# A graph-attention and expert kernel: expert jobs as one list over all passes, and weights loaded with whole rows per partition

## The chip, the cores and the metric

The kernel runs on one core of a Trainium2 chip. A core has a matrix engine (TensorE, PE in the profile; its weight loads are PEld), three further engines (VectorE or DVE, ScalarE or ACT, GpSimd or POOL), a queue engine that only issues transfers (SyncE or SP), and 16 DMA engines that move data between the chip's memory (DRAM here) and the core's own memory. Matrix results land in a small accumulator memory (PSUM). Each engine works through its own instructions in order and waits at semaphores for the others. The metric is the device time of one execution in microseconds (us); lower is better.

## The reference, cut to what matters

A graph layer is followed by a layer of eight experts. There are 6,250 nodes of 256 values, 100,000 edges, 8 experts with weights of 256 x 1024 and 1024 x 256 and a capacity of 977 nodes each. All is float32.

```python
h = layernorm(x)
messages = (h @ W_forward.T)[src] * direction[:, 0:1] + (h @ W_reverse.T)[src] * direction[:, 1:2]
scores = leaky_relu(einsum('ef,hf->eh', messages, attn), 0.2)
e = exp(scores - scores.max(0))
norm = e / (segment_sum(e, dst)[dst] + 1e-10)
x = x + concat_heads(segment_sum(messages * norm[:, hd:hd+1], dst))

t = layernorm(x)
probs = softmax(t @ gate_w + gate_b);  idx = argmax(probs);  prb = max(probs)
pos = number of earlier nodes with the same expert;  kept = pos < C
buf[idx, pos] = t                                   # only where kept
hmid = relu(einsum('ecd,edf->ecf', buf, w1) + b1)
ybuf = einsum('ecf,efd->ecd', hmid, w2) + b2
x = x + nan_to_num(ybuf[idx, pos] * prb * kept)
```

The order of the 256 inner values (`d`) and of the 1024 middle values (`f`) plays no part in the two expert products, as long as both factors of a product use the same order.

## The kernel before, in words

**Edge phase.** The edges, sorted by target node, are cut into 131 groups of 6 x 128, two groups to a batch, 66 batches. For batch `b`, `gathers` (POOL) fetches a row of `node_tab` for every edge, three batches ahead; `messages` (DVE, and one exp on ACT) forms the messages and the exponentials, `products` (DVE) multiplies them, and `windows` (PE) sums them by target with a 0/1 matrix as the stationary operand; the sums are stored by SP. When a chunk of four node tiles is complete, `route` normalises it, adds it to `x`, computes the layer norm and the gate, and gives each node a row in its expert's part of `buf`; POOL later scatters the rows there.

**Experts.** The rows of each expert come in five passes of 128, 256, 256, 256 and 128 rows (`PASS`), so that experts can begin before all nodes are routed: pass 0 when its nodes are scattered, and so on. A job is one pass of one expert; there are 40. `experts(p)` is a generator for one pass: it fetches rows and both weight matrices of experts 0 and 1, then for each expert

- `columns` turns the rows `xe` with PE transposes into `xT` (L1188, through `px`);
- `ph` (L1211): w1's columns are the stationary operand, `xT` is the moving one, 16 products per job; ACT adds the bias `b1t`, applies relu and writes `hf` (L1214);
- rows and w1 of the expert two further on are fetched (`fetch_rows`, `fetch_w1`), and the columns of the next expert are made;
- `py` (L1225): `hf` is the stationary operand, w2 the moving one; then w2 of the expert two further on is fetched (`fetch_w2`), DVE adds `b2` and cleans NaNs, and SP stores `y` to `ybuf`.

The two last experts of a pass fetch nothing; the first fetches of the next pass are in its own generator. `w1t` and `w2t` have two buffers each. Every matrix product in float32 shows as two matmul and weight-load pairs in the profile, so `ph` of a job is 32 pairs.

**Order.** The schedule is written out by hand: the main loop over batches calls `messages`, `windows`, a share of expert pieces, `products`, `windows`, a share, `route` pieces and `gathers` in turn. `step_experts` takes pieces from the generators of started passes until a credit of 4.3 us is used up; each `yield` gives the cost of a piece. After the last batch (near 1704 us) all remaining passes are worked off in one loop; after every third piece it fetches outputs (`fetch_outputs`: POOL gathers `ybuf` rows for two node tiles, SP loads the residual `xr`) and finishes earlier ones (`finish`: ACT, DVE and a store by SP). The outputs of a pass's nodes are fetched once the following pass is done.

**Layouts.** The layout of w1 in `fetch_w1` is

```python
w1[e].rearrange("(c p) f -> p c f", p=P)   # partition p holds rows p and 128+p, 4 KB each
w2[e].rearrange("(c p) d -> p c d", p=P)   # partition p holds rows p, 128+p, ...: 8 rows of 1 KB
```

so the stationary operand of `ph`, `w1t[:, d, f * P:(f + 1) * P]`, is 128 neighbouring values in each partition. The biases `b1` are loaded as 64 rows of 128 and transposed on PE to `b1t`, with one column per expert and block of 128 middle values.

Of the kernel before, what the change touches and what calls it, by code (L numbers as in the profile page):

```python
# [8 lines left out]
F32 = mybir.dt.float32  # L9
I32 = mybir.dt.int32  # L10
AF = mybir.ActivationFunctionType
# [3 lines left out]
P = 128  # L15
# [504 lines left out]
def kernel(  # L520
# [27 lines left out]
    nc = tc.nc  # L548
    N, D = x.shape
# [307 lines left out]
    nc.scalar.dma_start(gb, bass.AP(tensor=gate_b.tensor, offset=gate_b.offset, ap=[[0, P], [1, E]]))  # L857
    b2b = ep.tile([P, E, D], F32, name="b2b")
    nc.scalar.dma_start(b2b, bass.AP(tensor=b2.tensor, offset=b2.offset, ap=[[0, P], [D, E], [1, D]]))
    b1t = ep.tile([P, E * FC], F32, name="b1t")  # L860
    with tc.tile_pool(name="pb1", bufs=1) as pb1, \
            tc.tile_pool(name="psb", bufs=1, space=bass.MemoryType.PSUM) as psb:
        b1n = pb1.tile([E * FC, P], F32, name="b1n")
        nc.scalar.dma_start(b1n, b1.rearrange("e (c p) -> (e c) p", p=P))
        pbt = psb.tile([P, E * FC], F32, name="pbt")
        nc.tensor.transpose(pbt, b1n, ident[:E * FC, :E * FC])
        nc.vector.tensor_copy(b1t, pbt)

        ii = pb1.tile([P, NT], I32, name="ii")
        nc.gpsimd.iota(ii[:, :E], pattern=[[-1, E]], base=E, channel_multiplier=0)  # L870
        rank = ep.tile([P, E], F32, name="rank")
        nc.vector.tensor_copy(rank, ii[:, :E])
        ij = pb1.tile([P, NT], I32, name="ij")
        nc.gpsimd.iota(ij, pattern=[[P, NT]], base=NSLOT, channel_multiplier=1)
        own = ep.tile([P, NT], F32, name="own")
        nc.vector.tensor_copy(own, ij)
        valid = ep.tile([P, NT], F32, name="valid")
        nc.vector.tensor_scalar(valid, own, float(NSLOT + N), None, op0=OP.is_lt)
# [23 lines left out]
    with tc.tile_pool(name="p2", bufs=2) as p2, tc.tile_pool(name="p4", bufs=1) as p4, \  # L902
# [94 lines left out]
        taken = {"before": None, "z": 0}  # L997

        def windows(b, g):

# [164 lines left out]
        def fetch_w1(e):  # L1165
            w1t = wpool.tile([P, DC, FF], F32, name="w1t")
            nc.sync.dma_start(w1t, w1[e].rearrange("(c p) f -> p c f", p=P))
            return w1t

        def fetch_w2(e):  # L1170
            w2t = wpool.tile([P, FC, D], F32, name="w2t")
            nc.sync.dma_start(w2t, w2[e].rearrange("(c p) d -> p c d", p=P))
            return w2t

        def fetch_rows(p, e):
            S = PASS[p]
            J = S // P
            a = e * TOT + OFF[p]
            xe = p5.tile([P, 2, D], F32, name="xe", bufs=3)[:, :J, :]
            x_loads.append(nc.sync.dma_start(xe, buf[a:a + S, :].rearrange("(p j) d -> p j d", j=J)))  # L1180
            return xe

        def columns(p, xe):
            J = PASS[p] // P
            px = ps2.tile([P, DC, 2 * P], F32, name="px")[:, :, :PASS[p]]
            for j in range(J):
                for d in range(DC):
                    nc.tensor.transpose(px[:, d, j * P:(j + 1) * P], xe[:, j, d * P:(d + 1) * P], ident)  # L1188
            xT = p5.tile([P, DC, 2 * P], F32, name="xT")[:, :, :PASS[p]]
            nc.scalar.copy(xT, px)  # L1190
            return xT

        def experts(p):

            S = PASS[p]
            J = S // P
            FB = 512 // S
            w1s, w2s, xs = {}, {}, {}
            for e in (0, 1):
                xs[e], w1s[e], w2s[e] = fetch_rows(p, e), fetch_w1(e), fetch_w2(e)  # L1200
            yield 0.0
            xT = columns(p, xs.pop(0))
            yield 0.43 * J
            for e in range(E):
                w1t, w2t = w1s.pop(e), w2s.pop(e)
                hf = p5.tile([P, FC, 2 * P], F32, name="hf")[:, :, :S]
                for f0 in range(0, FC, FB):
                    ph = ps2.tile([P, FB, S], F32, name="ph", tag="acc", bufs=3)
                    for f in range(f0, f0 + FB):
                        for d in range(DC):  # L1210
                            nc.tensor.matmul(ph[:, f - f0, :], w1t[:, d, f * P:(f + 1) * P], xT[:, d, :],  # L1211
                                             start=(d == 0), stop=(d == DC - 1))
                    for f in range(f0, f0 + FB):
                        nc.scalar.activation(hf[:, f, :], ph[:, f - f0, :], AF.Relu,  # L1214
                                             bias=b1t[:, e * FC + f:e * FC + f + 1])
                    yield 0.85 * FB * J
                if e + 2 < E:
                    xs[e + 2], w1s[e + 2] = fetch_rows(p, e + 2), fetch_w1(e + 2)
                if e + 1 < E:
                    xT = columns(p, xs.pop(e + 1))  # L1220
                    yield 0.43 * J
                py = ps2.tile([P, 2, D], F32, name="py", tag="acc", bufs=3)[:, :J, :]
                for j in range(J):
                    for f in range(FC):
                        nc.tensor.matmul(py[:, j, :], hf[:, f, j * P:(j + 1) * P], w2t[:, f, :],  # L1225
                                         start=(f == 0), stop=(f == FC - 1))
                    if j + 1 < J:
                        yield 3.4
                if e + 2 < E:
                    w2s[e + 2] = fetch_w2(e + 2)  # L1230
                y = p5.tile([P, 2, D], F32, name="y")[:, :J, :]
                nc.vector.tensor_add(y, py, b2b[:, e, :].unsqueeze(1).to_broadcast([P, J, D]))  # L1232
# [5 lines left out]
                nc.sync.dma_start(ybuf[a:a + S, :].rearrange("(p j) d -> p j d", j=J), y)  # L1238
                yield 3.4

        def settle(n0, n1):
# [43 lines left out]


        SHARE = 8.6
        routing, passes, todo = [], [], []
        held = []
        credit = 0.0  # L1290
        next_c, next_p = 0, 0
# [38 lines left out]
        started = {}  # L1330
        for b in range(NB + 1):
            for p in [p for p, at in started.items() if b >= at]:
                passes.append(experts(p))
                del started[p]
            if b < NSLOT // 512:
                clear(buf, 512 * b)
                clear(ybuf, 512 * b)
            if b < NB:
                messages(b)
            if b:  # L1340
                windows(b - 1, order[b - 1][0])
            step_experts(SHARE / 2)
            if b < NB:
                products(b)
            if b and len(order[b - 1]) > 1:
                windows(b - 1, order[b - 1][1])
            step_experts(SHARE / 2)
            while next_c < len(chunks) and done_at[next_c] < b:
                routing.append(routes_of(next_c))
                next_c += 1  # L1350
            step_routing(3)
            pool_work.extend(held)
            held = todo[:]
            del todo[:]
            if b + 3 < NB:
                gathers(b + 3)
            if not pool_work and not held and not todo:
                for p in wait_pass:
                    started[p] = b + 2
                del wait_pass[:]  # L1360
# [2 lines left out]
            step_routing(1)  # L1363
        for put in pool_work + held + todo:
            put()
        for p in list(started) + wait_pass:
            passes.append(experts(p))
        ends = [0] + [t for t in LASTS[:-1]] + [NT - 1]
        fetch = []
        for q in range(NP):  # L1370
# [3 lines left out]
        settle(1, EARLY + 1)  # L1374
        settle(EARLY + 1, NT)
        settle(0, 1)
        left = NP - len(passes)
        work = [t for q in range(max(left - 1, 0)) for t in fetch[q]]
        for q, gen in enumerate(passes):
            pieces = 0  # L1380
            for cost in gen:
                pieces += 1
                if pieces % 3 == 0:
                    if len(fetched) > 1 or fetched and not work:
                        finish()
                    if work:
                        fetch_outputs(work.pop(0))
            work += fetch[left + q - 1]
        for tiles in work + fetch[NP - 1]:
            if len(fetched) > 1:  # L1390
                finish()
# [58 lines left out]
```

## Time and profile before

| | us |
|---|---|
| median of 3 runs | 2086.88 (2086.45 to 2089.06) |
| profiled execution, its own time | 2076.85 |
| its span | 2075.1 |
| PE busy in the span | 1176.9 (57%) |
| PE weight loads | 971.2 (47%) |
| DVE busy | 969.5 (47%) |
| POOL busy | 841.0 (41%) |
| ACT busy | 288.2 (14%) |
| mean granted PE clock | 0.762 of full speed |
| moved by DMA | 248.03 MB, 119 to 120 GB/s in the mean |

Lines of the profile start with a time in us from the start of the span and a duration, or with a stretch; "L1211" is line 1211 of the kernel, and `out<-in` names the tiles written and read. "SPq" is a transfer issued by SP; a DMA in the chain of waits lasts from its issue to its landing. In square brackets stands how long the engine had been idle before, and what ended the wait. The ends of matmuls are modelled, so steady rates are read from a row of many in succession.

### The profile page before, as it was taken

What the parts mean: (1) busy time and instruction counts of PE and PEld (TensorE: products, weight loads), DVE (VectorE), ACT (ScalarE), POOL (GpSimd) and SP (SyncE); (2) the same over time, 40 slices, a digit from 0 to 9 for tenths busy, and PEclk for the clock granted to TensorE, in tenths of its full rate; (3) what the DMA queues carried; (4) which work ended last, traced back from release to release, by engine and by line L of the source; (5) the groups of instructions that cost most, each with busy time, mean ns of one, the idle gap of its engine ahead of it and who ended that gap; (6) DMA issues with size and microseconds to landing.
All of it is one profiled execution on the core that took longest, in us unless ns stands there. A gap on an engine that the chain in (4) does not pass through costs nothing.

```text
span 2075.1 us, 16070 instructions
## 1 busy us (share of the span) xinstructions
PE 1176.9 (57%) x5000; PEld 971.2 (47%) x5000; DVE 969.5 (47%) x2074; ACT 288.2 (14%) x755; POOL 841.0 (41%) x896
## 2 busy tenths in 40 slices
PE   6421345443443763646436666467556789899760
PEld 5320333332332652535325555355445678788650
DVE  7640455463463561636544566375454643131224
ACT  2100000010010110201011111110110123232221
POOL 0075655536626445353734355455355301010112
PEclk9755766766776875867657787688677889999995
DMA  6222343332222642522243343343332337384773
GB/s 208 83 58 67 99 119 116 118 110 60 61 64 62 202 136 65 175 77 75 67 126 103 105 134 103 97 112 106 89 107 54 114 111 252 137 273 147 245 234 112
DMA packets 164365, 248.03 MB, mean 120 GB/s; under 512 B 19971, under 2 KB 128014, under 8 KB 164142
## 3 DMA queue, kind: packets, MB, share of 16 engines
q1 hardware_dynamic: 131466, 176.86, 26.0%
q0 software_dynamic: 29728, 67.35, 13.6%
q10 hardware_dynamic: 3076, 2.69, 0.4%
q8 instruction: 42, 0.69, 0.1%
q14 instruction: 53, 0.43, 0.1%
HBM read 181.85 MB, written 64.98 MB: 119 GB/s over the span
## 4 chain that ended last, share of the span: by engine, by line
PE 20%; DVE 11%; issue 10%; DMA 7%; another core or an unknown queue 3%; ACT 1%; POOL 1%; SPq 0%; DVEq 0%; ACTq 0%; POOLq 0%
PE py L1225 8%; PE ph L1211 8%; PE pv L1009 3%; DMA part<-sums 2%; DMA w1t<-in_L_ffn_w_dram 2%; DVE v L992 1%; DMA yg<-ybuf,to_get 1%; DVE m L967 1%; DVE rv L965 1%; DMA out_dram<-o 1%; PE pv L1018 1%; DMA sums<-r 1%; DVE hot L982 1%; DVE gt L960 1%
## 5 line engine op out<-in xcount | busy, mean ns | idle before, releaser
L944 POOL DMA_INDIRECT gt<-node_tab,srci x782 | 740.8, 947 | 730.7 <-DVE sc L970 500.8
L1009 PE MATMUL pv<-v,hot 128*128 128x260 f32 x1564 | 460.1, 453 | 307.7 <-issue 149.5
L1009 PEld LDWEIGHTS pv<-v,hot 128*128 128x128 f32 x1564 | 356.5, 232 | 393.5 <-issue 204.5
L1225 PE MATMUL py<-w2t,hf 128*128 128x256 f32 x1024 | 258.5, 407 | 76.5 <-ACT hf L1214 52.8
L1211 PE MATMUL ph<-xT,w1t 128*128 128x256 f32 (+1 forms) x1280 | 261.8, 362 | 45.4 <-issue 29.5
L1211 PEld LDWEIGHTS ph<-xT,w1t 128*128 128x128 f32 x1280 | 226.5, 209 | 74.8 <-issue 44.0
L1225 PEld LDWEIGHTS py<-w2t,hf 128*128 128x128 f32 x1024 | 206.8, 206 | 115.7 <-ACT hf L1214 55.3
L992 DVE TENSOR_TENSOR v<-m,fixed 128x3072 f32<-128x3072 f32 (+1 forms) x66 | 218.7, 3314 | 8.0 <-remote 1.8
L982 DVE TENSOR_TENSOR hot<-fixed,local 128x1536 f32<-128x1536 f32 (+1 forms) x66 | 114.2, 1730 | 205.4 <-remote 137.6
L1018 PE MATMUL pv<-v,zt 128*128 128x260 f32 x226 | 83.2, 453 | 161.9 <-DVE zt L1017 122.8
L1265 POOL DMA_INDIRECT yg<-ybuf,to_get x49 | 49.4, 1009 | 289.3 <-DMA ybuf<-y 134.5
L1232 DVE TENSOR_TENSOR y<-py,b2b 128x512 f32<-128x512 f32 (+1 forms) x40 | 23.3, 583 | 305.8 <-PE py L1225 292.7
L1214 ACT ACTIVATE hf<-ph,b1t 128x256 f32<-128x256 f32 (+1 forms) x320 | 116.4, 431 | 331.7 <-PE ph L1211 236.9
L1018 PEld LDWEIGHTS pv<-v,zt 128*128 128x128 f32 x226 | 46.3, 218 | 179.1 <-DVE zt L1017 130.5
L1021 ACT COPY r<-pv 128x260 f32<-128x260 f32 x131 | 47.5, 368 | 536.3 <-issue 460.6
L1136 POOL DMA_INDIRECT buf<-h,to_put x49 | 48.6, 991 | 87.7 <-DVE kept L1158 73.1
L960 DVE TENSOR_TENSOR gt<-gt,fixed 128x816 f32<-128x816 f32 (+1 forms) x66 | 65.5, 993 | 34.5 <-DMA gt<-node_tab,srci 27.3
L967 DVE TENSOR_TENSOR m<-gt,rv 128x408 f32<-128x408 f32 x131 | 75.5, 576 | 4.6
L965 DVE TENSOR_TENSOR rv<-gt,fixed 128x408 f32<-128x408 f32 x131 | 76.2, 581 | 2.2
L991 DVE COPY fixed<-v 128x48 f32<-128x48 f32 (+1 forms) x66 | 13.8, 209 | 122.3 <-ACT v L980 89.6
L980 ACT ACTIVATE v<-sc 128x48 f32<-128x48 f32 (+1 forms) x66 | 16.0, 243 | 390.9 <-DVE sc L978 174.0
L920 PE MATMUL pm<-ident,top_s 128*128 128x128 f32 x56 | 12.0, 332 | 76.9 <-DVE top_s L926 57.8
(208 smaller groups left out, 860.7 us busy)
## 6 DMA issues: line engine op xcount, KB each, us to landing
w1t<-in_L_ffn_w_dram SPq DMA_DIRECT2D x40, 1024.0 KB
w2t<-in_L_ffn_w_dram SPq DMA_DIRECT2D x40, 1024.0 KB
sums<-r SPq DMA_DIRECT2D x113, 125.9 KB
gt<-node_tab,srci POOLq DMA_INDIRECT x782
buf<-zeros SPq DMA_DIRECT2D x16, 512.0 KB
ybuf<-zeros SPq DMA_DIRECT2D x16, 512.0 KB
part<-sums SPq DMA_DIRECT2D x12, 520.0 KB
x_d<-x SPq DMA_DIRECT2D x12, 512.0 KB
```

The costliest lines, as they stand in the source:

```text
L944: nc.gpsimd.indirect_dma_start(out=gts[b][:, i - i0, :], out_offset=None, in_=node_tab, in_offset=bass.IndirectOffsetOnAxis(ap=srci[:, i:i ...
L960: nc.vector.tensor_mul(fw, fw, fac[:, 0, :n].unsqueeze(2).to_broadcast([P, n, MS]))
L965: nc.vector.tensor_mul(rv[:, :k, :], gt[:, a0:a1, MS:ROW], fac[:, 1, a0:a1].unsqueeze(2).to_broadcast([P, k, MS]))
L967: nc.vector.tensor_add(m[:, a0:a1, :], fw[:, a0:a1, :], rv[:, :k, :])
L982: nc.vector.tensor_tensor(hot[:, :n, :], lane_p.unsqueeze(1).to_broadcast([P, n, P]), local[:, i0:i1].unsqueeze(2).to_broadcast([P, n, P]) ...
L992: nc.vector.tensor_mul(v[:, :n, 0:H * O].rearrange("p n (h o) -> p n h o", h=H), m[:, :n, 0:O].unsqueeze(2).to_broadcast([P, n, H, O]), w[ ...
L1009: nc.tensor.matmul(pv, hot[:, i - i0, :], v[:, i - i0, :], start=(i == tiles[0]), stop=(i == tiles[-1] and before is None))
L1018: nc.tensor.matmul(pv, z[:, k, :], before, start=False, stop=True)
L1211: nc.tensor.matmul(ph[:, f - f0, :], w1t[:, d, f * P:(f + 1) * P], xT[:, d, :], start=(d == 0), stop=(d == DC - 1))
L1214: nc.scalar.activation(hf[:, f, :], ph[:, f - f0, :], AF.Relu, bias=b1t[:, e * FC + f:e * FC + f + 1])
L1225: nc.tensor.matmul(py[:, j, :], hf[:, f, j * P:(j + 1) * P], w2t[:, f, :], start=(f == 0), stop=(f == FC - 1))
L1265: nc.gpsimd.indirect_dma_start(out=yg[:, n, :], out_offset=None, in_=ybuf, in_offset=bass.IndirectOffsetOnAxis(ap=to_get[:, n0 + n:n0 + n ...
```

## The change

There are five edits.

1. One generator `experts()` goes through all 40 jobs. Job `i` fetches w1 and w2 of job `i + 2` also across the border between passes. It waits (`yield None`) until the pass of its job is released; rows are fetched only for released passes (`taken["released"]`). The columns of the next job are made before `py` also across a border, if the rows have been fetched.
2. w1 and w2 are loaded so that partition `p` holds whole neighbouring rows: two rows of w1 (8 KB in one piece) and eight rows of w2 (8 KB in one piece).
3. To match, the stationary operands are taken with a step: `w1t[:, d, f::FC]` (step 8) for `ph` and `xe[:, j, d::DC]` (step 2) for the transposes. `hf` and w2 then agree without further steps.
4. `b1` is loaded directly into `b1t` with `b1.rearrange("e (p c) -> p e c", c=FC)`, without the transpose.
5. The first weights are fetched when experts are first called in the main loop, after batch 12; the outputs' loop counts pieces over all passes.

```diff
-    b1t = ep.tile([P, E * FC], F32, name="b1t")
-    with tc.tile_pool(name="pb1", bufs=1) as pb1, \
-            tc.tile_pool(name="psb", bufs=1, space=bass.MemoryType.PSUM) as psb:
-        b1n = pb1.tile([E * FC, P], F32, name="b1n")
-        nc.scalar.dma_start(b1n, b1.rearrange("e (c p) -> (e c) p", p=P))
-        pbt = psb.tile([P, E * FC], F32, name="pbt")
-        nc.tensor.transpose(pbt, b1n, ident[:E * FC, :E * FC])
-        nc.vector.tensor_copy(b1t, pbt)
+    b1t = ep.tile([P, E, FC], F32, name="b1t")
+    nc.scalar.dma_start(b1t, b1.rearrange("e (p c) -> p e c", c=FC))
+    with tc.tile_pool(name="pb1", bufs=1) as pb1:
...
+        jobs = [(p, e) for p in range(NP) for e in range(E)]
+        w1s, w2s, xs = {}, {}, {}
+
+        def fetch_w1(i):
+            if i < len(jobs):
+                w1s[i] = wpool.tile([P, DC, FF], F32, name="w1t")
+                nc.sync.dma_start(w1s[i], w1[jobs[i][1]].rearrange("(p c) f -> p c f", c=DC))
+
+        def fetch_w2(i):
+            if i < len(jobs):
+                w2s[i] = wpool.tile([P, FC, D], F32, name="w2t")
+                nc.sync.dma_start(w2s[i], w2[jobs[i][1]].rearrange("(p c) d -> p c d", c=FC))
+
+        def fetch_rows(i):
+
+            if i < len(jobs) and i not in xs and jobs[i][0] < taken["released"]:
...
-                    nc.tensor.transpose(px[:, d, j * P:(j + 1) * P], xe[:, j, d * P:(d + 1) * P], ident)
+                    nc.tensor.transpose(px[:, d, j * P:(j + 1) * P], xe[:, j, d::DC], ident)
...
-        def experts(p):
+        def experts():
+
+
+            for i in (0, 1):
+                fetch_w1(i)
+                fetch_w2(i)
+            xT = None
+            for i, (p, e) in enumerate(jobs):
...
+                while taken["released"] <= p:
+                    yield None
+                for q in (i, i + 1):
+                    fetch_rows(q)
+                if xT is None:
+                    xT = columns(i)
+                    yield 0.43 * J
...
-                            nc.tensor.matmul(ph[:, f - f0, :], w1t[:, d, f * P:(f + 1) * P], xT[:, d, :],
+                            nc.tensor.matmul(ph[:, f - f0, :], w1t[:, d, f::FC], xT[:, d, :],
                                              start=(d == 0), stop=(d == DC - 1))
...
-                if e + 2 < E:
-                    xs[e + 2], w1s[e + 2] = fetch_rows(p, e + 2), fetch_w1(e + 2)
-                if e + 1 < E:
-                    xT = columns(p, xs.pop(e + 1))
+                fetch_rows(i + 2)
+                fetch_w1(i + 2)
+                xT = None
+                if i + 1 in xs:
+                    xT = columns(i + 1)
                     yield 0.43 * J
...
-                if e + 2 < E:
-                    w2s[e + 2] = fetch_w2(e + 2)
+                fetch_w2(i + 2)
...
         def step_experts(share):
             nonlocal credit
             credit = min(credit + share, share)
-            while passes and credit > 0:
-                cost = next(passes[0], None)
+            while credit > 0 and b > 12:
+                cost = next(ffn, None)
                 if cost is None:
-                    passes.pop(0)
-                else:
-                    credit -= cost
+                    break
+                credit -= cost
...
-        for q, gen in enumerate(passes):
-            pieces = 0
-            for cost in gen:
-                pieces += 1
-                if pieces % 3 == 0:
-                    if len(fetched) > 1 or fetched and not work:
-                        finish()
-                    if work:
-                        fetch_outputs(work.pop(0))
-            work += fetch[left + q - 1]
+        work, pieces, counted = [], 0, 0
+        for cost in ffn:
+
+            while counted < taken["passes"] - 1:
+                work += fetch[counted]
+                counted += 1
+            pieces += 1
+            if pieces % 3 == 0:
+                if len(fetched) > 1 or fetched and not work:
+                    finish()
+                if work:
+                    fetch_outputs(work.pop(0))
+        for q in range(counted, NP - 1):
+            work += fetch[q]
```

More of the change, by code (lines that the diff above doesn't have):

```diff
@@ L995, in products @@
                 w[:, :n, :].unsqueeze(3).to_broadcast([P, n, H, O]))
-        taken = {"before": None, "z": 0}
+        taken = {"before": None, "z": 0, "released": 0, "passes": 0}
         def windows(b, g):
@@ L1163, in end_pass @@
             nc.vector.tensor_tensor(done, done, kept, OP.min)
[L1165 to L1186, printed above, removed]
+        jobs = [(p, e) for p in range(NP) for e in range(E)]
[8 more added lines that the diff above has]
+                nc.sync.dma_start(w2s[i], w2[jobs[i][1]].rearrange("(p c) d -> p c d", c=FC))
@@ new lines, in fetch_rows, with columns @@
+        def fetch_rows(i):
+            if i < len(jobs) and i not in xs and jobs[i][0] < taken["released"]:
+                p, e = jobs[i]
+                S = PASS[p]
+                J = S // P
+                a = e * TOT + OFF[p]
+                xs[i] = p5.tile([P, 2, D], F32, name="xe", bufs=3)[:, :J, :]
+                x_loads.append(nc.sync.dma_start(xs[i], buf[a:a + S, :].rearrange("(p j) d -> p j d", j=J)))
+        def columns(i):
+            S = PASS[jobs[i][0]]
+            xe = xs[i]
+            px = ps2.tile([P, DC, 2 * P], F32, name="px")[:, :, :S]
+            for j in range(S // P):
@@ L1187, in columns @@
                 for d in range(DC):
-                    nc.tensor.transpose(px[:, d, j * P:(j + 1) * P], xe[:, j, d * P:(d + 1) * P], ident)
-            xT = p5.tile([P, DC, 2 * P], F32, name="xT")[:, :, :PASS[p]]
+                    nc.tensor.transpose(px[:, d, j * P:(j + 1) * P], xe[:, j, d::DC], ident)
+            xT = p5.tile([P, DC, 2 * P], F32, name="xT")[:, :, :S]
             nc.scalar.copy(xT, px)
             return xT
-        def experts(p):
[L1195 to L1205, printed above, removed]
+        def experts():
[4 more added lines that the diff above has]
+            for i, (p, e) in enumerate(jobs):
+                S = PASS[p]
+                J = S // P
+                FB = 512 // S
+                while taken["released"] <= p:
[5 more added lines that the diff above has]
+                    yield 0.43 * J
+                w1t, w2t = w1s.pop(i), w2s.pop(i)
@@ L1210, in experts @@
                         for d in range(DC):
-                            nc.tensor.matmul(ph[:, f - f0, :], w1t[:, d, f * P:(f + 1) * P], xT[:, d, :],
+                            nc.tensor.matmul(ph[:, f - f0, :], w1t[:, d, f::FC], xT[:, d, :],
                                              start=(d == 0), stop=(d == DC - 1))
                     for f in range(f0, f0 + FB):
-                        nc.scalar.activation(hf[:, f, :], ph[:, f - f0, :], AF.Relu,
-                                             bias=b1t[:, e * FC + f:e * FC + f + 1])
+                        nc.scalar.activation(hf[:, f, :], ph[:, f - f0, :], AF.Relu, bias=b1t[:, e, f:f + 1])
                     yield 0.85 * FB * J
-                if e + 2 < E:
-                    xs[e + 2], w1s[e + 2] = fetch_rows(p, e + 2), fetch_w1(e + 2)
-                if e + 1 < E:
-                    xT = columns(p, xs.pop(e + 1))
+                fetch_rows(i + 2)
[3 more added lines that the diff above has]
+                    xT = columns(i + 1)
                     yield 0.43 * J
@@ L1238, in experts @@
                 nc.sync.dma_start(ybuf[a:a + S, :].rearrange("(p j) d -> p j d", j=J), y)
+                if e == E - 1:
+                    taken["passes"] = p + 1
                 yield 3.4
@@ L1287 @@
         SHARE = 8.6
-        routing, passes, todo = [], [], []
+        routing, todo = [], []
+        ffn = experts()
         held = []
@@ L1332 @@
             for p in [p for p, at in started.items() if b >= at]:
-                passes.append(experts(p))
+                taken["released"] = p + 1
                 del started[p]
@@ L1365 @@
             put()
-        for p in list(started) + wait_pass:
-            passes.append(experts(p))
+        taken["released"] = NP
         ends = [0] + [t for t in LASTS[:-1]] + [NT - 1]
@@ L1376 @@
         settle(0, 1)
-        left = NP - len(passes)
-        work = [t for q in range(max(left - 1, 0)) for t in fetch[q]]
-        for q, gen in enumerate(passes):
-            pieces = 0
-            for cost in gen:
-                pieces += 1
-                if pieces % 3 == 0:
-                    if len(fetched) > 1 or fetched and not work:
-                        finish()
-                    if work:
-                        fetch_outputs(work.pop(0))
-            work += fetch[left + q - 1]
+        work, pieces, counted = [], 0, 0
[11 more added lines that the diff above has]
+            work += fetch[q]
         for tiles in work + fetch[NP - 1]:
```

## The prediction

> **What bounds the kernel now.** I read the busy time by stretch first, then the chain of work that ended last, then the instructions in order of time around the places that the chain names. Stretches (start:end, length, busy us of PE, weight loads, DVE, ACT, POOL, then granted clock, DMA share, GB/s):
>
> ```profile
> 1704.00:1801.00 97.00, 97.00 (x450) 84.94 (x450) 25.83 (x74) 27.31 (x64) 8.68 (x9) 0.97 0.51 172
> 1801.00:1927.00 126.00, 117.44 (x546) 102.28 (x544) 27.82 (x49) 35.62 (x84) 11.55 (x12) 0.96 0.62 205
> 1927.00:2014.00 87.00, 65.06 (x400) 58.23 (x400) 22.77 (x49) 26.08 (x84) 12.72 (x12) 0.92 0.83 274
> ```
>
> From 1704 us to 2014 us only experts' jobs are left: the end of pass 2, pass 3 (256 rows a job) and pass 4 (128 rows). TensorE is full in the first two stretches; in the third it is not, and the DMA share is 0.83. Before 1704 us experts are filled in beside the edge phase, and TensorE is busy 55 to 62% there. The chain, at its two breaks and in between:
>
> ```profile
> 1794.33 6.92 PE py L1225 x32
> 1804.07 6.57 DMA w1t<-in_L_ffn_w_dram
> 1810.77 9.41 PE ph L1211 x32
> 1820.62 6.91 PE py L1225 x32
> 1827.53 6.91 PE ph L1211 x32
> ...
> 1919.95 6.92 PE py L1225 x32
> 1929.69 6.18 DMA w1t<-in_L_ffn_w_dram
> 1936.01 6.51 PE ph L1211 x32
> 1942.73 3.46 PE py L1225 x16
> 1946.19 3.58 PE ph L1211 x32
> ```
>
> A 256-row product of 32 matmul and weight-load pairs takes 6.91 us, 216 ns a pair; a 128-row `ph` takes 3.58 us, 112 ns a pair. A pass that starts waits for its first `w1t`, and its first `ph` then runs on a lowered clock (9.41 and 6.51 us). In pass 4 it is SP that is late:
>
> ```profile
> 1955.30 0.44 SPq L1172 DMA_DIRECT2D w2t<-in_L_ffn_w_dram  x1
> 1964.21 0.33 SPq L1238 DMA_DIRECT2D ybuf<-y  x1
> 1966.01 0.48 SPq L1180 DMA_DIRECT2D xe<-buf  x1
> 1966.59 0.38 SPq L1167 DMA_DIRECT2D w1t<-in_L_ffn_w_dram  x1
> ```
>
> The store of `y` (ready at 1955.4) leaves only at 1964.2, after the gathers of `ybuf` issued until 1958.7; rows and weights of later jobs stand behind it. From its first `ph` (1936.0) to its end (2013.8) pass 4 takes about 9.7 us a job, where TensorE needs 3.58 + 0.25 + 3.46 = 7.3.
>
> [...] The change makes the stationary operand of `ph` step 8 floats (32 bytes) and that of the transposes `px` 2 floats (8 bytes). [...] The trace shows 240 to 430 GB/s in single microseconds with either matrix in flight, so 1 KB rows of `w2` cost little, and longer rows alone move nothing large. Two views bear on the stride. Eight bytes in a weight load (`raw_a`, min/median/max) against none (`fs`), and DVE reductions without a step, then with 16 bytes:
>
> ```profile
> L766 PEld LDWEIGHTS pti<-ident,raw_a x14: 196/226/226, 85.9 to 90.5; 128*128 128x128 f32 x14
> L766 PEld LDWEIGHTS pti<-ident,fs x7: 182/225/231, 81.6 to 88.0; 128*128 128x128 f32 x7
> ...
> 95.97 0.95 DVE L806 TENSOR_REDUCE wrong<-local 128x1 f32<-128x782 f32 x1
> 97.78 0.27 DVE L810 TENSOR_REDUCE wrong<-high 128x1 f32<-128x131 f32 x1
> 714.91 0.33 DVE L926 TENSOR_REDUCE top_s<-gmax 128x4 f32<-128x104 f32 x1
> 1687.47 0.62 DVE L926 TENSOR_REDUCE top_s<-gmax 128x4 f32<-128x264 f32 x1
> ```
>
> Eight bytes cost nothing, so I cost `px` at nothing. DVE goes from (0.95-0.27)/651 = 1.04 ns an element to (0.62-0.33)/160 = 1.81 ns [...].
>
> **The change, part by part.** No run shows a weight load with 32 bytes of step[...] a pair takes about 229 ns. All sums are against the profiled execution's 2076.85 us (span 2075.1).
>
> *256-row `ph`.* (229-216) x 32 = 0.4 us a job; 15 such jobs run after 1704 us: **+6**. The cover is the matmul of 216 ns; without it each job costs more, as under the second rival.
>
> *Start of pass 3.* The end of `py` at 1801.25 to the end of the first `ph` at 1820.2 is 18.9 us; inside a pass `px` and `ph` take 7.3. Weights come two jobs ahead across the border and rows are there (all are released), so nothing is late and the clock stays up: **-11.6**.
>
> *Pass 4.* Now 87.0 us from 1926.87 to 2013.8. After: 8 x (32 x 0.229 + 0.25 + 3.46) = 88.3. The wait at its start goes and the slower loads fill its place. SP's store of `y` still waits for gathers and later `w1t` still stand behind it, but a job of 11 us gives more time than one of 9.7: I add 2 for it. **+3**.
>
> *Edge phase, pass 0.* (229-112) x 32 = 3.7 us x 8 jobs = 30 us of TensorE. Its cover is TensorE's idle time beside DVE and POOL, and it is not whole:
>
> ```profile
> 704.10 0.42 DVE L1232 TENSOR_TENSOR y<-py,b2b 128x256 f32<-128x256 f32 x1 [16.39 <-PE py L1225]
> ```
>
> Here DVE stands still for `py`, and the messages and products of the next edge batch are queued behind it; ACT's exp is likewise behind `hf`. Elsewhere (789 to 819 us) TensorE issues a matmul only every 1.7 to 2.4 us and the load vanishes in the gaps. I take 0.4 of it: **+12** (bounds 0 and 30). Pass 1 and the first job of pass 2: 9 x 0.4 x 0.4 = **+1.5**.
>
> *Starts of passes 0 to 2.* TensorE waited 2.05, 2.25 and 4.82 + 1.53 us for weights and rows. Weights of pass 0 are fetched far earlier (four loads, with the edge batches' stores behind them for a few us, while nothing waits for these stores). The transposes of pass 2's first job move two windows ahead. Of 10.6 us I take 0.6: **-6**.
>
> *Bias.* Before, a transpose and a copy on DVE wait for `b1n`:
>
> ```profile
> 101.94 0.34 PE L866 MATMUL pbt<-ident,b1n 64*128 64x64 f32 x1 [9.32 <-DMA b1n<-in_L_ffn_b_dram]
> 103.16 1.11 POOL L944 DMA_INDIRECT gt<-node_tab,srci  x1 [2.96 <-DVE lead L1150]
> ```
>
> The first gather waits for `lead`, which is behind that copy; 1.67 us of wait and the copy go: **-2**. The new load has 1024 pieces of 32 bytes, but is first read at about 697 us, so it costs nothing.
>
> *Fetching of outputs.* Pieces are counted over all passes instead of per pass: the same gathers, some one piece earlier or later; and the 61 us after the last `py` stay. 0.
>
> Sum: 6 - 11.6 + 3 + 12 + 1.5 - 6 - 2 = **+3**, so 2080 for the profiled execution. The median of the runs (2086.88) stands 10 above the profiled one; with the same 10 I forecast **2090**.
>
> **The rivals.**
> *The stride costs nothing.* For it: TensorE's weight load need not behave as DVE's reader; 8 bytes cost nothing. Against: [...] DVE's 1.81 ns. Then +6, +12 and +1.5 go; pass 4 is bound by DMA: 274 GB/s x 87 us = 24 MB now, 4 MB of it loaded earlier, 20 MB at 298 GB/s (its rate from 1936 to 2000) is 66 us, -21; if SP's waits hold it, only -10. In all -30 to -41: 2046 to 2057.
> *The loads outgrow the matmuls.* One mechanism, in the same place, which ends slower: from a load of about 216 ns every further ns is paid in each of the 15 x 32 pairs of full TensorE as well; it decides from about 220 ns. At three times (325 ns a pair): 15 x 3.5 = 52, pass 4 113 us or +26, edge phase 22 + 13, less 20: +93, 2180. At four times (432 ns): 104 + 53 + 41 + 31 - 20 = +209, 2296. [...] against: DVE pays only 1.7 times.
> *The change doesn't do what it says,* because rows or a held buffer keep the next pass back as the weights did: in the order of instructions `px` of pass 3 stands before the last `py` of pass 2, so the wait could only be for `xe`, which has 14 us. It would take back the 11.6: 2102. I hold it in the upper part of my own case.
>
> **How the numbers follow.** [...] 0.66 (with the third rival inside), own range 2075 to 2107; no cost 0.15; three times or more 0.19. The range reaches down over the second case and up to a load of about 2.6 times (2150); it leaves out the rest of the last. A measurement of this kernel can tell about 0.2% (4 us) from no change. In my case I give 0.25 faster, 0.28 same, 0.47 slower; times 0.66, plus 0.15 faster and 0.19 slower: 0.31, 0.19, 0.50.
>
> **What would show it.** Pairs of `ph` in pass 4 at about 229 ns (7.3 us for 32) and 7.1 to 7.6 us in pass 3, against 3.6 and 6.9 if the stride is free, and over 10 in both if loads outgrow matmuls. No wait for `w1t` near 1800 and 1925 us and no `ph` of 9.4 us. `px` unchanged. First gather about 2 us earlier. Wrong I would be above all by the size of the strided load, then by the share of pass 0 that the edge phase hides.

## The result and the profile after

The changed kernel takes **2103.48 us** (median of 20 runs, 2096.15 to 2115.86). The kernel before, run beside it, takes 2095.93 us (20 runs, 2084.11 to 2104.83). The ratio is **1.0047, with a 95% interval of 1.0027 to 1.0067**: slower by 9.9 us (5.7 to 14.0). (The ratio is not that of the two medians, which lie 7.6 us apart.) The profiled execution took 2103.40 us, with a span of 2101.6 us.

The stretches from the last routing to the last `py`, in the columns of the prediction (start:end, length, busy us of PE, weight loads, DVE, ACT, POOL, granted clock, DMA share, GB/s). First the rest of pass 2, then pass 3, then pass 4 of the changed kernel:

```profile
1728.00:1830.50 102.50, 102.50 (x457) 95.84 (x457) 26.05 (x74) 27.82 (x65) 9.08 (x9) 0.97 0.58 199
1830.50:1951.20 120.70, 120.56 (x545) 113.56 (x543) 27.97 (x48) 35.45 (x84) 11.38 (x12) 1.00 0.62 212
1951.20:2040.60 89.40, 89.35 (x398) 85.88 (x397) 22.93 (x49) 24.90 (x83) 11.98 (x12) 1.00 0.64 228
```

Pass 3 is 5 us shorter (120.7 against 125.6, counted from the end of pass 2's last `py`). Pass 4 is 2.4 us longer (89.4 against 87.0), but it is another pass 4: before, TensorE was busy for 65.06 us of 87.00 and the DMA engines for 0.83 of the time; now TensorE is busy for 89.35 of 89.40 us, and the DMA share is 0.64. The chain of waits shows the same at the two borders (time, length, engine, product, line, number of pairs):

```profile
1823.59 6.91 PE py L1234 x32
1830.50 7.68 PE ph L1220 x32
1838.18 0.46 PE px L1191 x4
1838.64 6.91 PE py L1234 x32
...
1944.27 6.91 PE py L1234 x32
1951.17 7.54 PE ph L1220 x32
1958.93 3.46 PE py L1234 x16
1962.39 7.50 PE ph L1220 x32
```

No transfer of `w1t` stands in the chain any more, and no `ph` of 9.41 us; the first product of pass 3 starts where the last one of pass 2 ends. In exchange every 256-row `ph` takes 7.68 us (240 ns a pair) instead of 6.91, every 128-row one 7.50 (234 ns) instead of 3.58, and four transposes take 0.46 to 0.47 us instead of 0.44. Instructions in order of time near the first gather:

```profile
100.49 0.17 DVE L1148 TENSOR_SCALAR lead<-lead 128x8 f32<-128x8 f32 x1
101.04 1.11 POOL L941 DMA_INDIRECT gt<-node_tab,srci  x1 [1.10 <-DVE fixed L955]
```

The wait for `b1n` is gone, and the first gather starts at 101.0 us instead of 103.2.

### The profile page after: what moved, and what is told of

Read it like the earlier page. It is cut to its first block, busy times and chain, and to the rows that moved or that the text cites. A ratio compares the mean times of both kernels' runs of the same rounds, so it can differ in the third digit from the quotient of the medians.

```text
span 2101.6 us, 16058 instructions
## 1 busy us (share of the span) xinstructions
PE 1240.2 (59%) x4999; PEld 1061.2 (50%) x4999; DVE 970.2 (46%) x2073; ACT 287.8 (14%) x755; POOL 842.4 (40%) x896
## 2 busy tenths in 40 slices
DMA packets 124365, 248.03 MB, mean 118 GB/s; under 512 B 20995, under 2 KB 88014, under 8 KB 113902
## 4 chain that ended last, share of the span: by engine, by line
PE 34%; issue 25%; DVE 22%; another core or an unknown queue 9%; DMA 6%; ACT 2%; POOL 1%; SPq 0%; DVEq 0%; ACTq 0%; POOLq 0%
PE ph L1220 11%; PE py L1234 10%; PE pv L1006 6%; DVE v L989 4%; DMA part<-sums 2%; PE pv L1015 2%; DVE m L964 2%; DVE hot L979 2%; DVE rv L962 2%; DVE gt L957 2%; PE pl L1080 1%; PE pn L717 1%; DMA sums<-r 1%; POOL gt L941 1%
## 5 line engine op out<-in xcount | busy, mean ns | idle before, releaser
L1220 PE MATMUL ph<-xT,w1t 128*128 128x256 f32 (+1 forms) x1280 | 325.6, 414 | 7.4 <-issue 5.5
L1220 PEld LDWEIGHTS ph<-xT,w1t 128*128 128x128 f32 x1280 | 316.5, 335 | 13.8 <-issue 4.3
L962 DVE TENSOR_TENSOR rv<-gt,fixed 128x408 f32<-128x408 f32 x131 | 76.1, 581 | 2.5 <-DVE m L964 0.2
```

The costliest lines, as they stand in the source:

```text
L962: nc.vector.tensor_mul(rv[:, :k, :], gt[:, a0:a1, MS:ROW], fac[:, 1, a0:a1].unsqueeze(2).to_broadcast([P, k, MS]))
L1220: nc.tensor.matmul(ph[:, f - f0, :], w1t[:, d, f::FC], xT[:, d, :], start=(d == 0), stop=(d == DC - 1))
```

## The experiments

They were made in three groups, each with its own runs of the kernel before: a median of 2093.69 us in the first (21 runs), 1724.14 in the second (21), 2080.96 in the third (32). In the second the whole edge phase is some 350 us shorter, for every kernel; the last section comes back to it. So the time of each run is compared only within its group, and split in two at the last routing, which is the last start of the matmul on `pre` in the profile. The stretch after it hardly depends on the group (before: 2075.1 - 1704.0 = 371.1 us, and 1719.8 - 1350.8 = 369.0 in the second group's profile of the unchanged kernel, `before_again`). Runs of the second group are set against 369.0, those of the other two against 371.1, since the third has no profile of the kernel before. What lies ahead of it scatters from run to run and is taken as the rest: (ratio - 1) times the median of before, less the difference of the stretches. A rest so carries the whole interval of its run, and 2 to 3 us from the single profiles.

| run (group) | whole against before, us (95%) | stretch after the last routing, us | its difference | rest: edge phase |
|---|---|---|---|---|
| the change itself | +9.9 (5.7 to 14.0) | 373.3 | +2.2 | +7.7 |
| list_only (1) | -22.0 (-29.3 to -14.9) | 349.1 | -22.0 | 0.0 |
| layout_only (1) | +35.0 (27.6 to 42.3) | 390.9 | +19.8 | +15.2 |
| list_step2 (1) | -24.1 (-31.0 to -17.2) | 351.7 | -19.4 | -4.7 |
| list_step4 (1) | +11.7 (7.5 to 15.9) | 369.1 | -2.0 | +13.7 |
| wide_pass0 (2) | -14.8 (-18.3 to -11.4) | 354.5 | -14.5 | -0.3 |
| wide_later (2) | +3.8 (1.6 to 6.0) | 373.2 | +4.2 | -0.4 |
| list_free_y (2) | -27.9 (-31.9 to -23.8) | 343.1 | -25.9 | -2.0 |
| after_again (3) | +7.1 (2.9 to 11.2) | 373.5 | +2.4 | +4.7 |
| list_again (3) | -20.2 (-27.7 to -12.7) | 350.6 | -20.5 | +0.3 |
| wide_pass0_again (3) | -15.2 (-20.4 to -10.0) | 351.7 | -19.4 | +4.2 |
| list2_free_y (3) | -35.8 (-42.9 to -28.9) | 344.4 | -26.7 | -9.1 |

**My theory:** the job list takes the two waits at the starts of passes away, and the strided weight load of `ph` gives back as much or more. **The rivals:** the stride is free, or it multiplies the load beyond the matmuls; or the list does not do what it says.

### Each half of the change alone

`list_only` has the job list, with all layouts of before:

```diff
-nc.sync.dma_start(w1s[i], w1[jobs[i][1]].rearrange("(p c) f -> p c f", c=DC))
+nc.sync.dma_start(w1s[i], w1[jobs[i][1]].rearrange("(c p) f -> p c f", p=P))
-nc.sync.dma_start(w2s[i], w2[jobs[i][1]].rearrange("(p c) d -> p c d", c=FC))
+nc.sync.dma_start(w2s[i], w2[jobs[i][1]].rearrange("(c p) d -> p c d", p=P))
-nc.tensor.matmul(ph[:, f - f0, :], w1t[:, d, f::FC], xT[:, d, :],
+nc.tensor.matmul(ph[:, f - f0, :], w1t[:, d, f * P:(f + 1) * P], xT[:, d, :],
```

and likewise for the transposes and `b1t`. `layout_only` is the reverse: the generators by pass of before, with the new layouts and steps.

> The job list alone, with the matrices, biases and stationary operands laid out as before. If the step of the weight loads is what the changed kernel pays for: 32 pairs of ph back at 6.9 us (256 rows) and 3.6 us (128 rows), no wait at the start of pass 3 (11 us gained), pass 4 of 66 to 77 us instead of 87, the edge phase within 5 us of before; 25 to 38 us faster than before (ratio 0.982 to 0.988). If the list itself costs (weights that are fetched early collide with the edge phase): not faster than before, with the edge phase some 10 us or more longer. If SP's waits for the stores of y hold pass 4: it stays at 77 to 87 us, and the gain is only 11 to 20 us.

> The layouts alone (whole rows per partition, steps 8 and 2, biases without transpose), with the generators per pass of before. If the step is the cost: ph at 7.7 us (256 rows) and 7.5 us (128 rows), 16 x 0.8 = 12 us in passes 2 and 3, the wait for w1t at the starts of passes 3 and 4 still there (6 us), pass 4 of 95 to 100 us, the edge phase 10 to 20 us longer; in all 30 to 45 us slower than before (1.014 to 1.022). If whole rows help the transfers enough to count: w1t lands in clearly less than 6 us at the starts of passes, and the loss is under 20 us.

Measured: the list alone 2071.14 us, ratio 0.9895 (0.986 to 0.9929); the layouts alone 2124.10 us, ratio 1.0167 (1.0132 to 1.0202). So the two halves are both large and of opposite sign. The loss of the layouts is as expected; the list's gain of 22 us is below the 25 to 38 expected for the case that the step is all that the change pays for. The chain of waits of `layout_only` at the same two borders:

```profile
1824.42 6.92 PE py L1221 x32
1834.16 5.82 DMA w1t<-in_L_ffn_w_dram
1840.11 9.24 PE ph L1207 x32
...
1954.69 6.92 PE py L1221 x32
1964.43 5.30 DMA w1t<-in_L_ffn_w_dram
1969.87 7.90 PE ph L1207 x32
```

The waits are back with the generators, so it is the list that removes them. With whole rows the landings in these profiles are 0.75 and 0.88 us shorter (5.82 and 5.30 against 6.57 and 6.18); one profile of each kernel does not show that the rows are the reason. And although all transfers together take 124365 packets instead of 164365, no more gain from the longer rows can be seen.

The stretches of `list_only`, pass 3 and pass 4:

```profile
1821.08:1936.30 115.22, 114.08 (x545) 100.11 (x544) 27.81 (x48) 35.62 (x84) 11.75 (x12) 1.00 0.67 222
1936.30:2012.40 76.10, 62.78 (x398) 56.80 (x397) 23.36 (x48) 25.52 (x83) 11.61 (x12) 0.96 0.80 268
```

Without the stride pass 3 takes 115.2 us instead of 125.6, and pass 4 takes 76.1 instead of 87.0, with TensorE busy for 62.8 of them. The change has the list too, and yet its passes take 120.7 and 89.4 us: 5.5 and 13.3 us of the list's gain are lost there.

### How the cost depends on the step

The job list again, with `w2` in pieces of two rows (2 KB) and `ph` with a step of 2 values (8 bytes), or in pieces of four rows and a step of 4 (16 bytes); w1, `px` and the direct load of `b1` as in the change:

```diff
-nc.tensor.matmul(ph[:, f - f0, :], w1t[:, d, f::FC], xT[:, d, :],
+nc.tensor.matmul(ph[:, f - f0, :], w1t[:, d, f // 2 * 256 + f % 2:(f // 2 + 1) * 256:2], xT[:, d, :],
```

> The changed kernel with ph's stationary operand at a step of 2 values (8 bytes) in place of 8: blocks of 256 middle values, w2 in pieces of 2 KB, w1 still in 8 KB, biases loaded to match. [...] pairs of 216 and 112 ns, all as in the job list alone (within 5 us), with the first gather 2 us earlier than before. If every step costs in proportion: pairs of 128-row jobs between 120 and 150 ns and pass 4 some 5 us longer than with the list alone.

> The same with a step of 4 values (16 bytes)[...]. [...] pairs of 240 ns (256 rows) and 234 ns (128 rows) as with 8, and the time of the changed kernel within 0.4%. If the cost grows with the distance: pairs clearly below, for instance 216 and 150 to 180 ns, and a time between those of steps 2 and 8.

Measured: 2070.26 us, ratio 0.9885 (0.9852 to 0.9918), with a step of 2; 2103.32 us, ratio 1.0056 (1.0036 to 1.0076), with a step of 4. The weight loads of `ph` and `px` from 1200 us on (minimum, median and maximum in ns). Kernel before, no step:

```profile
L1211 PEld LDWEIGHTS ph<-xT,w1t x960: 186/190/338, 1219.6 to 2010.0; 128*128 128x128 f32 x192
L1188 PEld LDWEIGHTS px<-ident,xe x100: 138/141/230, 1253.8 to 2002.7; 128*128 128x128 f32 x100
```

Step 2 in `ph`, 2 in `px`:

```profile
L1221 PEld LDWEIGHTS ph<-xT,w1t x960: 193/196/338, 1235.3 to 2009.7; 128*128 128x128 f32 x192
L1192 PEld LDWEIGHTS px<-ident,xe x100: 194/206/231, 1269.4 to 2002.4; 128*128 128x128 f32 x100
```

Step 4 in `ph`:

```profile
L1221 PEld LDWEIGHTS ph<-xT,w1t x960: 307/329/338, 1232.5 to 2024.8; 128*128 128x128 f32 x192
```

The change, step 8 in `ph`:

```profile
L1220 PEld LDWEIGHTS ph<-xT,w1t x960: 312/337/344, 1236.6 to 2036.6; 128*128 128x128 f32 x192
```

The records of loads overlap one another (the median load of `ph` in pass 4 of the kernel before takes 192 ns, where a pair takes 112), so the pace is read from the chain of waits, and above all from the 128-row `ph`, whose pairs grow with every step. Step 2, 128 rows; then step 4, 256 and 128 rows:

```profile
2006.30 3.76 PE ph L1221 x32
...
1926.08 7.47 PE ph L1221 x32
...
1940.69 7.36 PE ph L1221 x32
```

That is 112 ns a pair without a step (3.58 us for 32), 117.5 with 8 bytes (3.76), 230 with 16 bytes (7.36), 234 with 32 bytes (7.50). With 256 rows it is 216 without a step and with 8 bytes, 233 with 16 and 240 with 32. For 8 bytes neither expectation holds in full: they cost 5% with 128 rows (117.5 against 112 ns a pair), and nothing with 256 rows (216 ns both). Nearly all of the cost comes in one jump, between 8 and 16 bytes: the 128-row pair with 16 and 32 bytes takes 230/112 = 2.05 and 234/112 = 2.09 times as long as without a step. What makes the jump is not shown, and no step between 8 and 16 bytes was run.

So after the last routing all but 2.6 us of the loss by the layouts sit in the step of `ph`. With a step of 2 the whole rows of w1, the direct bias and a `w2` in 2 KB pieces are there, and the gain of the list is kept: the stretch is 351.7 us, against 349.1 with no step at all. The first gather, expected 2 us earlier, starts at 102.9 us here, hardly before the 103.2 of the kernel before.

### Pass 0 and the later passes

With the job list, a step of 8 in pass 0 alone, and in passes 1 to 4 alone; the other jobs take w2 as in the kernel before (`b1` is loaded in both orders):

```diff
-nc.tensor.matmul(ph[:, f - f0, :], w1t[:, d, f::FC], xT[:, d, :],
+nc.tensor.matmul(ph[:, f - f0, :], w1t[:, d, f::FC] if p == 0 else w1t[:, d, f * P:(f + 1) * P], xT[:, d, :],
```

> The changed kernel with the step of 8 in pass 0 alone; passes 1 to 4 take neighbouring columns and w2 as before. All that differs from the list alone lies in the edge phase. If the edge phase hides the slower loads only in part (0.4 of 30 us as predicted): 8 to 15 us slower than with the list alone, ratio to before 0.993 to 0.997. If the idle time of TensorE hides them: the time of the list alone (ratio 0.988 to 0.991). From 1730 us on both see the same stretch of 349 us after the last routing.

> The step of 8 in passes 1 to 4 and not in pass 0. If pass 0 costs 8 to 15 us in the edge phase: as much faster than the changed kernel, about even with before (ratio 0.997 to 1.001). If pass 0 is hidden: the time of the changed kernel (1.003 to 1.007). The stretch after the last routing is that of the changed kernel, 373 us.

> The job list with the stride of 8 in pass 0 alone. Its difference from the list alone on the same chip is what pass 0's stride costs in the edge phase (30 us of TensorE time): 12 us by the forecast's share of 0.4; 5 to 8 us by the one-look comparison of the last routings on the second chip; 0 if the idle time of TensorE hides it all. The stretch after the last routing stays within 6 us of the list alone.

Measured in the second group: 1710.32 us, ratio 0.9914 (0.9894 to 0.9934), with the step in pass 0; 1728.09 us, ratio 1.0022 (1.0009 to 1.0035), with it in the later passes. The later passes bring the stretch after the last routing to 373.2 us, the same as the change: everything that is lost there comes from them. For the edge phase the rest is -0.3 us with the step in pass 0, and -0.4 and -2.0 in the two kernels without it. By these rests, which are uncertain by 2 to 4 us each, the 31 us or so that the step adds on TensorE in pass 0 (an estimate from pass 4: 8 x (7.50 - 3.58)) are all or nearly all hidden in this group. The ratio of `wide_later` lies between its two cases and does not decide between them.

In the third group the same kernel, `wide_pass0_again`, has 2067.51 us, ratio 0.9927 (0.9902 to 0.9952), beside 2066.10 for the list alone. By the rests (+4.2 and +0.3) pass 0's step costs 3.9 us here; single pairs don't resolve it. Over the first and third groups and the change's own runs, the four runs of job lists with a step of 4 or 8 in pass 0 have rests of +7.7, +13.7, +4.7 and +4.2 (mean 7.6), the four without one of 0.0, -4.7, +0.3 and -9.1 (mean -3.4). By that the step costs some 11 us in the edge phase there, with an uncertainty of more than half of it, since each rest carries the 4 to 7 us of its interval. `layout_only`, with +15.2 and no list, fits to it. It is not pass 0 alone: three of the four also have the step in pass 1 and in the first job of pass 2. What pass 0 itself costs stays open, between nothing and some 12 us.

### What holds pass 4 without the stride

In `list_only` pass 4 takes 76.1 us, where TensorE needs 8 x 7.3 = 58. Its chain of waits, from the end of pass 3:

```profile
1938.24 4.35 DMA ybuf<-y
...
1944.75 6.32 DMA yg<-ybuf,to_get
...
1951.09 0.02 ACT yg L1290
...
1951.50 0.36 ACT xT L1197
...
1951.91 2.07 PE ph L1224 x16
```

A store of `y` must land before POOL gathers outputs; ACT waits for these, with `xT` of the next job behind it. On SP the next store of `y` waits for the gathers in turn. `list_free_y` is `list_only` with these two waits lifted where they are not needed: a gather for nodes of earlier passes reads no row of a later pass's store, and so neither has to wait for the other.

```diff
-nc.sync.dma_start(ybuf[a:a + S, :].rearrange("(p j) d -> p j d", j=J), y)
+st = nc.sync.dma_start(ybuf[a:a + S, :].rearrange("(p j) d -> p j d", j=J), y)
+for need, ins in yg_loads:
+    if p > need:
+        tc.declare_no_dep(st.ins, ins.ins, reason="rows of a later pass")
+y_stores.append((p, st))
```

and the same in `fetch_outputs` for gathers against earlier stores.

> The list alone, and stores of y no longer wait for gathers of earlier passes' rows of ybuf, nor such gathers for these stores. If SP's waits hold pass 4 at 76 us: it takes 60 to 68 us, and the kernel is 8 to 16 us faster than with the list alone (ratio to before 0.981 to 0.986). If DMA (12 MB of weights and the outputs) or the chain of gathers, ACT, DVE and stores holds it: 72 us or more, and the time of the list alone within 4 us.

SP's own waits during pass 4 (line, what it waited for: total us, times, longest). `list_only`:

```profile
SPq L1250 <- DMA yg<-ybuf,to_get: 30.4, 7, 7.7
SPq L1177 <- PE py L1238: 10.3, 4, 6.7
SPq L1250 <- DVE y L1248: 8.6, 3, 6.4
```

`list_free_y`:

```profile
SPq L653 <- DVE y L1245: 19.4, 3, 9.9
SPq L1178 <- PE py L1239: 10.7, 4, 6.7
SPq L1251 <- DVE y L1249: 10.0, 4, 6.9
```

SP's waits of 30.4 us for gathers are gone. Pass 4 falls to 70.8 us (1559.3 to 1630.1) and the stretch after the last routing to 343.1 us, 6 less than in `list_only`; ratio 0.9838 (0.9815 to 0.9862) in its group. In that same group `wide_pass0`, which has no step in `ph` in pass 4 and keeps these waits, takes 77.1 us for it (1572.9 to 1649.9). 70.8 lies between what the two cases expected (60 to 68, or 72 and more): the waits held pass 4, and something else holds it next. SP now waits for DVE instead, at the stores of outputs (L653) and of `y` (L1251), and behind these the rows of later jobs come late: three transfers of `xe` of 4.62, 8.87 and 4.37 us stand in the chain of this stretch. So the gathers held pass 4 by 5 to 6 us, not by all of the 18 that it stood above TensorE's need. The change has such waits on SP too (23.5 us in pass 4); they cost it nothing, because a job there takes TensorE 11.2 us and TensorE is busy for 89.35 of the 89.40 us.

### The change again, and a version that beats both

`after_again` is the change unchanged, `list_again` is `list_only`, both in the third group. `list2_free_y` is the list with a step of 2 in `ph` alone, the direct bias, w1 and `px` as before, and the free stores of `y`.

> The changed kernel beside the kernel before and the three below, on one chip. Stretch after the last routing: 373 to 374 us (369 to 371 before), whatever the chip, because it is set by the matrix engine's 15 full jobs, each 0.77 us longer, by the start of pass 3 (-11) and by pass 4 (+2). What the edge phase adds decides the rest: on a chip like that of the two mixed kernels +5 to +8 us, so a ratio of 1.004 to 1.007; if pass 0's stride costs nothing there, 1.001 to 1.002; on a chip like the first, 1.003 to 1.007 as before.

> The job list with all layouts as before. Theory (the list saves the start of pass 3 and part of pass 4, the strided weight load gives it back): 20 to 24 us shorter after the last routing, the edge phase within 5 us of before; in all -18 to -27 us. Rival (the gain on the first chip was partly a longer edge phase of the kernel before there): -10 us or less.

> The job list with a step of 2 values in ph alone (w2 in pieces of 2 KB, bias loaded directly, transposes and w1 as before), and the stores of y independent of output gathers of earlier passes. If the two savings add: 25 to 30 us shorter than before after the last routing, the first gather 2 to 3 us earlier, in all -24 to -35 us, a ratio of 0.983 to 0.989 on a chip of 2090 us. If the step of 2 costs in pass 4, where a load has no slack (117.5 against 112 ns a pair, 32 x 5.5 ns = 0.18 us a job), no more than 1.5 us of that is lost.

Measured: 2087.58 us (22 runs), ratio 1.0034 (1.0014 to 1.0054); 2066.10 us, ratio 0.9903 (0.9867 to 0.9939); 2047.41 us, ratio **0.9828 (0.9794 to 0.9861)**. The change is slower by about the same again; its stretch after the last routing is the same to 0.2 us. The list's gain repeats (-20.2 after -22.0). Pass 4 of `list2_free_y`:

```profile
1903.81:1974.42 70.61, 63.76 (x399) 58.24 (x397) 22.94 (x48) 25.34 (x83) 11.37 (x12) 0.95 0.83 289
```

70.6 us: the step of 2 leaves the gain of the free stores in place. Against the list alone 6.2 us are saved after the last routing; that its edge phase has a rest of -9.1 us is more than I can derive; the interval of its ratio alone is +-7 us.

## Why the prediction was right, and where its steps were wrong

The forecast was 2090, with 2040 to 2150 around it, and "slower" as its likeliest sign with half of the chance. The mechanism was right: the list removes the wait at the start of a pass, and the weight load with a step gives it back. The sum was too small: +3 us, below the interval of the measured +9.9 (5.7 to 14.0). After the last routing it had 2.8 - 8.4 + 3 = -2.6 us where +2.2 were measured, and that miss is the length of a strided pair (240 ns for 229). This part repeats (+2.4) and is known to about 2 us, which is what the kernel before itself differs by (371.1 and 369.0). The larger part of the difference, +7.7 of +9.9, lies in the edge phase, and its split is not settled. So that "slower" came true rests in part on terms that no run confirms, and in that part it is luck.

| term | forecast, us | measured, us | read from |
|---|---|---|---|
| rest of pass 2: longer `ph` | +2.8 (7 of the 15 jobs) | +5.0 | 102.2 (1728.3 to 1830.5) against 97.2 (1704.0 to 1801.2) |
| pass 3: start, and 8 longer `ph` | -11.6 + 3.2 = -8.4 | -4.9 | 120.7 against 125.6 |
| start of pass 3 alone | -11.6 | -10.8 | 18.9 to 8.1 us, its first strided `ph` and `px` included |
| pass 4 | +3 | +2.4 | 89.4 against 87.0 |
| after the last `py` | 0 | -0.3 | 61.0 against 61.3 |
| edge phase in all (+12 +1.5 -6 -2) | +5.5 | +7.7, again +4.7 | table of runs; each has an interval of +-4 |

- **256-row `ph`.** The step that failed is the length of a strided pair. The 229 ns were an estimate that leaned on DVE's 1.81 ns an element (x 128 = 232 ns) and on figures that no trace shows; that a weight load would follow DVE was not shown either. The pair takes 240 ns. The cover of 216 ns is there as I said, and it was passed, but by 24 ns and not by 13: 0.77 us a job instead of 0.4. Over 15 jobs this is +11.5 instead of +6. Nor does the longer matmul cover the load whole: with the same step a 128-row pair takes 234 ns and a 256-row pair 240. Where these 6 ns come from stays open.
- **`px` at nothing.** Wrong in kind, small in size: 8 bytes do cost. I compared loads in stretches where the granted clock was 0.50 (226 against 225 ns); in jobs, at 0.92 to 1.00 in the mean of a pass, the median goes from 141 to 207 ns. Four transposes go from 0.44 to 0.46 or 0.47 us, which is 0.3 to 0.5 us over 15 jobs. With `ph` it is 117.5 against 112 ns a pair.
- **Start of pass 3.** As forecast: the list removes the wait for w1, the raised clock stays (1.00 in pass 3; before, the first `ph` of pass 3 had 0.76 and that of pass 4 0.56), and nothing else is late. The measured 8.1 us hold 0.8 us for the step; without it they are the forecast's 7.3. The rival that rows or a held buffer keep the pass back is refuted in the changed kernel, where pass 3 has no idle PE (120.56 of 120.70).
- **Pass 4.** The total is right to 0.6 us, with the reason as given: the wait goes, and the longer `ph` (7.50 us for 3.58) fills its place. That it is so near is luck: the 2 us added for SP were not needed, since 8 x (7.50 + 0.23 + 3.46) = 89.5 is all of the 89.4, and they made up for a pair that was taken too short (88.3).
- **Edge phase.** The sum is right within its interval, but its terms are not confirmed. +12 and +1.5 for the step agree with the mean over the runs of the first and third groups (some 11); the one pair there with pass 0 alone gives 3.9, and the second group near 0, so my share of 0.4 is no property of the kernel alone. Nor are the gaps at 789 to 819 us, in which the load was to vanish, a property of the kernel. (1.7 to 2.4 us is the pause between two matmuls there, not the time from one to the next.) From 700 to 1300 us such pauses, put down to "issue", add up to 24.3 us ahead of `ph` in the first profile; none is listed there in the profile of the change or in `before_again`. For the list without a stride in pass 0 I had -6 (starts) and -2 (bias); the rests are 0.0, +0.3, -0.4 and -2.0 in the four kernels that still transpose the bias, and -4.7 and -9.1 in the two that load it directly. Most of the -6 is not to be seen. The bias's 2 us at the first gather are there in the mean only: it starts at 101.2 to 103.4 us in the five profiles that only transpose the bias (mean 102.5), and at 98.8 to 102.9 in the six that only load it directly (mean 100.6). Whether they reach the end stays open.
- **The absolute time.** The kernel before itself had a median of 2095.93 over 20 runs, 9 us above the three runs from which I started. Of the 13.5 us between 2090 and 2103.48 this is 9; the other 4.5 are what the two medians differ by (7.6) beyond the sum of +3.

**The rivals.** "The stride costs nothing" is refuted by the pairs of 234 and 240 ns. Its working for pass 4 with no cost of stride, though, holds: shorter by 10 us "if SP's waits hold it" is what `list_only` shows (-10.9), and lifting them brings 5 more. Its -21 was too much, since rows and other waits follow at 70.8 us, and so was its total of -30 to -41: the list alone has -22.0 and -20.2. "The loads outgrow the matmuls" is right in that a pair takes longer than the 216 ns of a 256-row matmul, but it takes 234 to 240 ns, and not the 325 or 432 of that estimate, 2.9 and 3.9 times the 112 ns of a pair without a step.

## What to carry to other kernels

Before a weight matrix is re-laid for longer DMA rows, look at the operand that TensorE then reads: here a step of 16 bytes doubled the 128-row matmul and load pair (112 to 230 ns), one of 8 bytes cost 5% (117.5), and a `w2` in pieces of two rows needs no more than that. A matmul covered the slower load only as far as it was itself long (216 ns with 256 rows): the 256-row products lost 0.77 us each, the 128-row ones 3.9. When two edits of opposite sign come together, run each alone: here -22 and +35 us lay under a difference of +10.

## What the runs showed of the hardware that I had not expected

The jump of the 128-row pair with the step: 117.5 ns at 8 bytes, 230 at 16, and little more at 32 (234), from 112 without one.

The other is the edge phase of the second group. The unchanged kernel reaches its last routing at 1350.8 us there, against 1704.0 in the first profile, while the stretch after it differs by 2 us. Groups of the edge phase (busy us, mean ns of one, then idle us before it, and what ended it), first profile of the kernel before:

```profile
L1009 PE MATMUL pv<-v,hot 128*128 128x260 f32 x1564 | 460.1, 453 | 307.7 <-issue 149.5 <-ACT r L1021 114.3 <-DVE v L992 37.7
L982 DVE TENSOR_TENSOR hot<-fixed,local 128x1536 f32<-128x1536 f32 (+1 forms) x66 | 114.2, 1730 | 205.4 <-remote 137.6 <-issue 37.9 <-PE ph L1211 27.4
```

The same kernel in the second group:

```profile
L1009 PE MATMUL pv<-v,hot 128*128 128x260 f32 x1564 | 432.8, 434 | 61.8 <-DVE v L992 48.7 <-issue 6.6 <-DVE kept L1156 6.5
L982 DVE TENSOR_TENSOR hot<-fixed,local 128x1536 f32<-128x1536 f32 (+1 forms) x66 | 114.2, 1730 | 1.7 <-PE pv L1009 1.7
```

The operations take the same time or nearly so (1730 ns, and 453 against 434 ns); what differs is idle time for which the profile knows no releaser within the kernel ("issue", "remote"): 149.5 us before TensorE's group and 137.6 + 37.9 = 175.5 before DVE's, against 6.6 and none that is listed in the second group. In the first profile PE, ACT and DVE stand still in single pieces of up to 38 us. The chip is not the difference: the second and the third group ran on the same one, with medians of 1724.14 and 2080.96 us for the unchanged kernel. No run tested a cause, and it stays open. `before_again` was meant to show whether the first profile of the kernel before was a short execution; with an edge phase 350 us shorter it could not. For reading such a kernel it means that a difference in its edge phase is only worth what repeated runs say, while the experts' stretch can be read from one profile to about 3 us (351.7 against 354.5 for the same kernel in two groups).
